# Last chunks without folds, coarser norm bound, nine early units and another split of the output stores in a fused attention and convolution kernel

## The chip, the cores and the metric

The kernel runs on one core of one Trainium2 chip, in float32. The metric is the device time of one launch in microseconds; the time of a version is the median of its runs.

## What is computed

The reference chains two layers over an image batch x of 2 images, 256 channels, 64 by 64 pixels:

```python
# layer 0: global attention, 8 heads of 32, over all 4096 pixels of an image
q = proj(Wq, bq) / sqrt(32); k = proj(Wk, bk); v = proj(Wv, bv)
fuse = softmax(q @ k.T) @ v
hybrid = conv1x1(concat([x, fuse]), Wf, bf)
x = hybrid * m + x * (1 - m)             # m: mask, 32x32 resized to 64x64
# layer 1
x = x * sigmoid(channel_mlp(x))
x = x + window_attention(x)              # 8x8 windows, 4 heads of 64
x = channel_shuffle(x, 4)
y = relu(bn(grouped_conv7x7(x, sa_w1)))  # 64 groups: 4 channels to 1
y = bn(grouped_conv7x7(y, sa_w2))        # 1 channel to 4
out = x * sigmoid(y)
```

## The kernel before, in words

**Start.** The images are cut into 16 chunks of 512 pixels (2 images, 8 chunks each). For each chunk TensorE computes q and k (line 435), ScalarE adds the bias and squares them (445 to 448), and VectorE takes the maximum of the squares over groups of 4 tokens (454). One chunk later `norms` (411 to 416) sums these maxima over the 32 rows of each head with a 0/1 matrix on TensorE (4 matmuls) and VectorE keeps the largest. The result bounds every score, and a flag (498) decides whether the exponentials need a shift; the two versions of the rest are built as `arm("a")` and `arm("b")`, and with these inputs the flag takes arm a, without the shift. Then the v projection runs (472).

**Attention.** `slots` lists image, chunk, half of the heads g and key block m: 64 slots for a chunk. In each slot TensorE computes scores (640), ScalarE exponentiates (653), TensorE multiplies by v (691), and VectorE adds the exponentials up (697). In all chunks but the last there are two chains of sums, one for even and one for odd m (`chains = 2`), joined at the end (699). `fold` (661) then packs the sums of a chunk, [128, 4, 512] for each g, with 24 DMAs on GpSimd into one tile (tag "w0"), so that the denominators need 3 terms of 4 small matmuls (725); in the last chunk, with one chain, they are computed from the sums themselves in 8 terms. Their reciprocal (752) goes to DRAM and comes back spread over the rows (737, 744), and VectorE multiplies the attention output by it (758). `at(delay, action)` puts such actions off by a number of slots.

**Stages.** The rest of layer 0 and layer 1 up to the shuffle of a chunk is the generator `stage`. It is advanced every fourth slot, so it runs beside the next chunk's attention. It begins with the 1x1 convolution (`hya`, 526), whose first half needs only x and whose second half needs the multiplied attention output `fa`, and it ends with rows written to the DRAM array `xs` (1020). The last chunk's stage has no attention beside it.

**Convolutions.** `convolve` is a generator as well. A unit u is 4 groups. An item of `items` is a unit with one or both images. For each item `conv1` (1088) and `conv2` (1113) run on TensorE, ScalarE makes the gate of it (1124, 1130), and `gate` (1136) multiplies it with x (1141) and stores it to the output: 12 DMAs for each image, dealt out over the issuing engines in `engines`; stores on ScalarE are held back and issued after the next item's ScalarE work (1159). After it come the loads of a later item's rows (`load_rows`, 1067) and of a later unit's weights (`load_w`, 1060). Image 0 is complete before the last chunk of image 1, so its first `EARLY` units (0 to 7) go as single-image items ahead of all that needs image 1; they fill TensorE in the last chunk's stage, one generator step at each `yield True` of `stage`, after two steps during the wait for the denominators (1261). `staged` is set when the last stage is over. Each image-1 row load waits for that stage's `xs` writes. The items are 8 singles of image 0, 6 singles of image 1 (units 2 to 7), units 8 to 15 with both images, and units 1 and 0 of image 1. Rows are loaded into 4 buffers in turn. `conv1` has one PSUM tile, so it starts when ScalarE has drained the one before (1096).

Each engine is given its instructions in a fixed order. DMAs are issued by SP, ScalarE and GpSimd, each also in order. In the built program the DMAs of SP and ScalarE share eight completion semaphores in turn and those of GpSimd have eight of their own; a DMA is not issued before the one that had its semaphore eight turns earlier has landed.

Of the kernel before, what the change touches and what calls it, by code (L numbers as in the profile page):

```python
# [31 lines left out]
DN = 8  # L32
EARLY = 8
HEADS1, HD1 = 4, 64
# [23 lines left out]
def conv_seq_kernel(ctx: ExitStack, tc: tile.TileContext, a, out):  # L58
# [311 lines left out]

    nm = const.tile([P, B * NCHUNK], F32, name="nm")
    flag = const.tile([1, 1], I32, name="flag")
    warm = const.tile([1, 1], F32, name="warm")
    with (
# [36 lines left out]
        def norms(i, tops):  # L411
            s = psum1(f"nrm_{i}")
            for n in range(2 * KC):
                s_ = s[32 * n : 32 * n + 32, 0 : CH // 4]
                nc.tensor.matmul(s_, headsum, tops[:, n, :], start=True, stop=True)
            nc.vector.tensor_reduce(nm[:, i : i + 1], s[:, 0 : CH // 4], AX.X, ALU.max)
# [6 lines left out]
        for i, (b, c) in enumerate(chunks):  # L423
            load_chunk()
            x = xs0[i]
            sq = st0.tile([P, 2 * KC, CH], F32, tag="sq", name=f"sq_{b}_{c}")
            tops = st0.tile([P, 2 * KC, CH // 4], F32, tag="top4", name=f"top4_{b}_{c}")
            for n, w in (("q", wq), ("k", wk)):
# [25 lines left out]
            nc.vector.tensor_reduce(  # L454
                tops, sq.rearrange("p g (n f) -> p g n f", f=4), AX.X, ALU.max
            )
            if i:
                norms(i - 1, last)
            last = tops
# [7 lines left out]
        for i, (b, c) in enumerate(chunks):  # L467
# [18 lines left out]
            if i == 0:  # L486
                norms(len(chunks) - 1, last)
                nc.vector.tensor_reduce(top, nm, AX.X, ALU.max)
            elif i == 1:

                nc.tensor.matmul(row[0:1, 0:P], top, ident, start=True, stop=True)
                qk2 = w0.tile([1, 2], F32, name="qk2")
                nc.vector.tensor_reduce(
                    qk2, row[0:1, 0:P].rearrange("p (i r) -> p i r", i=2), AX.X, ALU.max
                )
                prod = w0.tile([1, 1], F32, name="prod")
                nc.vector.tensor_mul(prod, qk2[:, 0:1], qk2[:, 1:2])
                nc.vector.tensor_scalar(flag, prod, (SAFE / SCALE0) ** 2, None, ALU.is_le)
            elif i == 2:


                s = psum1("bvf")
                for oc in range(KC):
                    for kc in range(KC):
                        nc.tensor.matmul(
                            s[:, oc : oc + 1],
                            wf[:, KC + kc, oc * P : (oc + 1) * P],
                            bv[:, kc : kc + 1],
                            start=(kc == 0),
                            stop=(kc == KC - 1),  # L510
                        )
                nc.vector.tensor_add(bf, s[:, 0:KC], bf)
# [17 lines left out]
    def pipeline(arm, shifted, pools):  # L530
# [145 lines left out]
        def products(i):  # L676
            b, c, g, m = slots[i]
            chains = 1 if (b, c) == (B - 1, NCHUNK - 1) else 2
            if m == 0:
                acc[0] = avp.tile([P, CH], F32, tag="av", name=f"av{arm}_{i}")  # L680
# [19 lines left out]
            if stop:  # L700
# [3 lines left out]
                nc.scalar.copy(f[:, g, :], av)  # L704
                if chains == 2:
                    fold(totals.pop((b, c, g)), b, c, g)
                if g == 0:
                    return
                both = [] if chains == 2 else [totals.pop((b, c, gg)) for gg in range(KC)]
                parts = folds.pop((b, c), [])  # L710
# [38 lines left out]
                late = EB + 1 if (b, c) == (0, 0) else 0  # L749
                wait = DN + 2 * (chains == 2)  # L750
                at(wait, denominators)
# [276 lines left out]

        items = [(u, (0,)) for u in range(EARLY)] + [(u, (1,)) for u in range(2, EARLY)]
        items += [(u, (0, 1)) for u in range(EARLY, NU)] + [(1, (1,)), (0, (1,))]  # L1030
        staged, held = [], deque()

        def convolve():
# [102 lines left out]
            def gate(k, zs):  # L1136
                u, images = items[k]
                for m, b in enumerate(images):
# [3 lines left out]

                    engines = (nc.gpsimd, nc.sync)
                    if k >= len(items) - 2:
                        engines = (nc.scalar, nc.sync)
                    elif staged and k < EARLY:
                        engines = (nc.gpsimd, nc.scalar)
                    stores = 0
# [18 lines left out]
            def more():  # L1167
                if staged and not xcs:
# [5 lines left out]
                    xcs.append(pool.tile([P, B * nb, UG, WP], F32, name=f"xl{arm}3"))  # L1174
                    load_rows(EARLY + 3)
                return bool(xcs)
# [9 lines left out]
            for k, (u, images) in enumerate(items):  # L1186
# [10 lines left out]
                if xcs or k + 4 < EARLY:  # L1197
                    load_rows(k + 4)

# [27 lines left out]
        for i, (b, c, g, m) in enumerate(slots):  # L1227
            now[0] = i
            if (b, c, g, m) == (B - 1, NCHUNK - 1, 0, 16):
                for _ in banded:  # L1230
                    pass
                conv = convolve()
                next(conv)
# [10 lines left out]
            if g == KC - 1 and m == NMB - 1:  # L1244
                late = EB + 4 if (b, c) == (0, 0) else 0
                at(DN + 8 + ((b, c) != (B - 1, NCHUNK - 1)) + late, lambda b=b, c=c: stages.append(stage(b, c)))
            run_later()
# [10 lines left out]
        while later:  # L1258
            now[0] += 1
            run_later()  # L1260
            if now[0] in (len(slots) + DN, len(slots) + DN + 1):
                next(conv)
# [91 lines left out]
```

## Time and profile before

| | us |
|---|---|
| median of 3 runs (2928.01 to 2930.89) | 2930.63 |
| profiled execution, own time | 2927.96 |
| its span, first to last instruction | 2926.2 |
| TensorE busy | 2873.4 (98%) |
| ScalarE busy | 2455.0 (84%) |
| VectorE busy | 2437.0 (83%) |
| GpSimd busy | 568.6 (19%) |

The span was cut for reading at the ends of stages: projections to 186 us, attention with stages from there to 2696, the last stage with single units to 2762, the remaining convolutions to 2910, and the last stores to 2926. A line of the timeline is start, duration, engine, source line, operation and tile, and in brackets the idle time before it with what ended it. "issue" there means that the engine waited for nothing that the profile shows. SPq and ACTq lines are the DMA issues on these queues; their length covers waits between the DMAs of one group.

### The profile page before, as it was taken

Reading aid. Unit: us, or ns where it says so; the run is one execution under the profiler, and the core shown is the slowest. Engines: PE = TensorE matmul, PEld = TensorE weight load, DVE = VectorE, ACT = ScalarE, POOL = GpSimd, SP = SyncE. Lnnn points to the kernel's source line nnn. Section 1 sums busy time; section 2 is a strip of 40 time slices with the busy share of each in tenths; the row PEclk is TensorE's granted clock in tenths of the full one; section 3 lists DMA queues with packets and bytes.
Section 4 is the critical chain, followed back from the end, with each engine's and each line's share of the span. In section 5 each row is a group of like instructions: output and inputs, shape, how many; then the busy total and the mean of one; then the engine's idle time right before and its main releaser. Section 6 shows DMA issues by size and latency. Waiting matters only on the chain.

```text
span 2926.2 us, 84951 instructions
## 1 busy us (share of the span) xinstructions
PE 2873.4 (98%) x36722; PEld 821.6 (28%) x36722; DVE 2437.0 (83%) x1356; ACT 2455.0 (84%) x4143; POOL 568.6 (19%) x929
## 2 busy tenths in 40 slices
PE   9999999999999999999999999999999999999897
PEld 3551122222222222222222222222222222223564
DVE  4339999899999999989989999999999998988211
ACT  5569989898989898989989898989898998978433
POOL 8111111111011212121111101111212121100356
PEclk9999999999999999999999999999999999999999
DMA  8545433333343434343333334343434343332564
GB/s 246 202 172 186 147 89 75 95 83 89 69 95 78 105 79 104 79 91 89 91 86 82 88 73 92 72 97 79 106 77 91 88 97 84 86 103 81 154 202 108
DMA packets 249364, 307.71 MB, mean 105 GB/s; under 512 B 124432, under 2 KB 141012, under 8 KB 248724
## 3 DMA queue, kind: packets, MB, share of 16 engines
q1 hardware_dynamic: 200996, 231.74, 27.8%
q0 software_dynamic: 40656, 67.09, 12.3%
q8 instruction: 291, 4.77, 0.7%
q10 hardware_dynamic: 7328, 3.36, 0.5%
q14 instruction: 93, 0.76, 0.1%
HBM read 221.88 MB, written 66.39 MB: 99 GB/s over the span
## 4 chain that ended last, share of the span: by engine, by line
PE 91%; DMA 3%; DVE 2%; issue 2%; ACT 1%; POOL 1%; SPq 0%; ACTq 0%; DVEq 0%; POOLq 0%
PE sa L640 34%; PE ava L691 33%; PE qka L526 4%; PE hya L526 3%; PE c1a L1088 2%; PE c2a L1113 2%; PE vwa L526 2%; PE opa L526 2%; PE v L472 2%; PE q L435 2%; PE k L435 1%; DVE suma L697 1%; DMA invs<-inva 1%; PE sca L878 1%; PE oa L972 1%
## 5 line engine op out<-in xcount | busy, mean ns | idle before, releaser
L653 ACT ACTIVATE ea<-sa 128x512 f32<-128x512 f32 (+1 forms) x3072 | 2037.1, 747 | 49.4 <-PE sa L640 22.6
L640 PE MATMUL sa<-qa,ka 32*64 32x512 f32 x16384 | 1146.6, 613 | 1.5 <-ACT vst L480 1.2
L697 DVE TENSOR_TENSOR suma<-suma,ea 128x2048 f32<-128x2048 f32 x480 | 1097.6, 2287 | 5.8 <-DVE suma L697 0.5
L691 PE MATMUL ava<-ea,va 128*32 128x512 f32 x8192 | 1091.1, 605 | 1.0
L697 DVE TENSOR_TENSOR odda<-odda,ea 128x2048 f32<-128x2048 f32 x420 | 959.7, 2285 | 46.0 <-ACT ea L653 45.9
L670 POOL DMA_DIRECT2D folda<-suma x360 | 252.7, 899 | 1787.7 <-DVE suma L699 1043.2
L640 PEld LDWEIGHTS sa<-qa,ka 32*64 32x64 f32 x16384 | 242.4, 129 | 785.5 <-ACT ea L653 716.5
L691 PEld LDWEIGHTS ava<-ea,va 128*32 128x32 f32 x8192 | 161.6, 108 | 834.0 <-issue 804.6
L697 DVE TENSOR_TENSOR suma<-ea,ea 128x2048 f32<-128x2048 f32 x32 | 73.2, 2286 | 58.8 <-ACT ea L653 58.8
L1161 POOL DMA_DIRECT2D out_dram<-za x180 | 101.7, 573 | 86.0 <-DVE za L1141 63.6
L526 PE MATMUL qka<-ua,qkv_w 128*32 128x512 f32 x1024 | 116.2, 592 | 0.3 <-DVE ua L834 0.3
L781 ACT ACTIVATE ta<-hya,bf 128x512 f32<-128x512 f32 x32 | 20.3, 685 | 108.9 <-PE hya L526 102.9
L1141 DVE TENSOR_TENSOR za<-za,xla 128x768 f32<-128x768 f32 x24 | 23.0, 959 | 100.6 <-ACT za L1130 88.7
L454 DVE TENSOR_REDUCE top<-sq 128x512 f32<-128x2048 f32 x16 | 36.6, 2285 | 79.3 <-ACT sq L448 79.3
L737 POOL DMA_DIRECT2D invs<-inva x62 | 34.3, 562 | 296.0 <-DVE inva L752 295.0
L899 ACT ACTIVATE ewa<-ewa,mxwa 128x64 f32<-128x64 f32 x256 | 85.5, 350 | 1.5 <-DVE mxwa L890 1.5
L1113 PE MATMUL c2a<-yca,wa 32*64 32x192 f32 (+1 forms) x2688 | 83.3, 384 | 0.7 <-issue 0.5
L785 DVE TENSOR_TENSOR ta<-ta,mca 128x512 f32<-128x512 f32 x32 | 22.0, 689 | 71.4 <-ACT ta L781 71.4
L1124 ACT ACTIVATE za<-c2a 128x384 f32<-128x384 f32 x64 | 27.9, 487 | 57.0 <-PE c2a L1113 30.1
L1088 PE MATMUL c1a<-xla,wa 128*32 128x192 f32 (+1 forms) x896 | 64.1, 435 | 11.6 <-issue 5.9
L857 ACT ACTIVATE qka<-qka,qkv_b 128x512 f32<-128x512 f32 x64 | 40.4, 685 | 40.8 <-PE qka L526 40.8
L1020 POOL DMA_DIRECT2D xs<-xo x94 | 72.0, 1017 | 11.0 <-DVE xo L1005 8.3
(143 smaller groups left out, 1724.7 us busy)
## 6 DMA issues: line engine op xcount, KB each, us to landing
ka<-ks SPq DMA_DIRECT2D x256, 256.0 KB
va<-vs SPq DMA_DIRECT2D x256, 256.0 KB
folda<-suma POOLq DMA_DIRECT2D x240, 64.0 KB, 3.1
folda<-suma POOLq DMA_DIRECT2D x120, 128.0 KB, 3.9
wa<-ws SPq DMA_DIRECT2D x17, 896.0 KB
ws<-zeros SPq DMA_DIRECT2D x16, 896.0 KB
xs<-xo POOLq DMA_DIRECT2D x78, 140.0 KB, 7.9
xla<-xs SPq DMA_DIRECT2D x24, 420.0 KB
```

What stands on the lines that cost most here:

```text
L435: nc.tensor.matmul(s[:, g, :], w[:, kc, g * P : (g + 1) * P], rhs, start=(kc == 0), stop=(kc == KC - 1),)
L526: nc.tensor.matmul(out[o : o + 32], weights[:, o : o + 32], x, start=start, stop=stop)
L640: nc.tensor.matmul(heads[j][o], k[r, cols][:, o], q[r, g, :], start=True, stop=not shifted)
L653: nc.scalar.activation(e[:, h, :], tile, AF.Exp, scale=SCALE0)
L670: nc.gpsimd.dma_start(dst[p : p + rows], total[rows * k : rows * k + rows, h, :], accum_op=ALU.add if k else ALU.bypass,)
L691: nc.tensor.matmul(av[r, :], v[:, m % PB, r], e[:, j, :], start=start, stop=stop)
L697: nc.vector.tensor_add(total, first.pop(m % chains, total), e)
L899: nc.scalar.activation(e[:, n, :], e[:, n, :], AF.Exp, bias=mx[:, n : n + 1], accum_out=rs[:, n : n + 1],)
L1020: eng.dma_start(x_s[b, n, p + r0 : p + r1].rearrange("r g w -> g r w"), xo[64 * h : 64 * h + 64, oc, r0 - WS * c : r1 - WS * c, :],)
L1088: nc.tensor.matmul(s[32 * j : 32 * j + 32, 0 : n * W], w[:, j, d, :], xs[k][:, 0:n, j, d : d + W], start=(d == 0), stop=(d == KS - 1),)
L1113: nc.tensor.matmul(tiles[j // 2][o, j % 2, 0 : n * W], w[r, d, o], y[r, 0:n, d : d + W], start=(d == 0), stop=(d == KS - 1),)
L1161: eng.dma_start(*args)
```

## The change

It touches four places.

- The squares are reduced over 16 tokens instead of 4, four chunks share one `tops` tile, and `norms` runs once for four chunks: 4 times instead of 16.
- `folded` replaces the test on `chains`: chunk 6 of image 1 keeps its two chains but is no longer folded, its denominators come from the sums, 2 slots earlier; the due time of its stage moves by one slot. `convolve` is started at slot 12 of the last chunk instead of 16.
- `EARLY` is 9: unit 8 becomes two single items. The last unit, 15, becomes two single items too. There is one more generator step during the last wait for denominators. At the staging, the rows of one image-1 item are loaded instead of four, and later ones at most one item for each gate until the ninth.
- Stores: of each three, two go to GpSimd and one to SP; none to ScalarE, except in the last two items (before: in items 4 to 7 and the last two).

```diff
-EARLY = 8
+EARLY = 9
...
-    nm = const.tile([P, B * NCHUNK], F32, name="nm")
+    nm = const.tile([P, B * NCHUNK // 4], F32, name="nm")
...
-                nc.tensor.matmul(s_, headsum, tops[:, n, :], start=True, stop=True)
+                nc.tensor.matmul(
+                    s_, headsum, tops[:, n].rearrange("p c n -> p (c n)"), start=True, stop=True
+                )
...
-            tops = st0.tile([P, 2 * KC, CH // 4], F32, tag="top4", name=f"top4_{b}_{c}")
+            if i % 4 == 0:
+                tops = st0.tile([P, 2 * KC, 4, CH // 16], F32, tag="top16", name=f"top16_{i}")
...
-                tops, sq.rearrange("p g (n f) -> p g n f", f=4), AX.X, ALU.max
+                tops[:, :, i % 4], sq.rearrange("p g (n f) -> p g n f", f=16), AX.X, ALU.max
             )
-            if i:
-                norms(i - 1, last)
+            if i and i % 4 == 0:
+                norms(i // 4 - 1, last)
...
-                norms(len(chunks) - 1, last)
+                norms(len(chunks) // 4 - 1, last)
...
+            folded = (b, c) < (B - 1, NCHUNK - 2)
...
-                if chains == 2:
+                if folded:
                     fold(totals.pop((b, c, g)), b, c, g)
...
-                both = [] if chains == 2 else [totals.pop((b, c, gg)) for gg in range(KC)]
+                both = [] if folded else [totals.pop((b, c, gg)) for gg in range(KC)]
...
-                wait = DN + 2 * (chains == 2)
+                wait = DN + 2 * folded
...
-        items += [(u, (0, 1)) for u in range(EARLY, NU)] + [(1, (1,)), (0, (1,))]
+        items += [(u, (0, 1)) for u in range(EARLY, NU - 1)]
+        items += [(NU - 1, (0,)), (NU - 1, (1,)), (1, (1,)), (0, (1,))]
...
-                    engines = (nc.gpsimd, nc.sync)
-                    if k >= len(items) - 2:
+                    engines = (nc.gpsimd, nc.gpsimd, nc.sync)
+                    if k == len(items) - 1:
                         engines = (nc.scalar, nc.sync)
-                    elif staged and k < EARLY:
-                        engines = (nc.gpsimd, nc.scalar)
+                    elif k == len(items) - 2:
+                        engines = (nc.scalar, nc.sync, nc.sync)
...
-                    load_rows(EARLY + 3)
+                    load_rows(EARLY)
...
-                    load_rows(k + 4)
+                    load_rows(min(len(xs) + (k >= EARLY - 1), k + 4))
...
-            if (b, c, g, m) == (B - 1, NCHUNK - 1, 0, 16):
+            if (b, c, g, m) == (B - 1, NCHUNK - 1, 0, 12):
...
-                at(DN + 8 + ((b, c) != (B - 1, NCHUNK - 1)) + late, lambda b=b, c=c: stages.append(stage(b, c)))
+                at(DN + 8 + ((b, c) < (B - 1, NCHUNK - 2)) + late, lambda b=b, c=c: stages.append(stage(b, c)))
...
-            if now[0] in (len(slots) + DN, len(slots) + DN + 1):
+            if len(slots) + DN <= now[0] <= len(slots) + DN + 2:
                 next(conv)
```

## The prediction

> **What bounds the kernel now.** I read the stage table (busy time by stretch) first, then TensorE's timeline at every stage where it isn't full, then the chain of waits there, then the queues that the change touches.
>
> ```profile
> 186.00:2525.00 2339.00, 2332.32 (x29461) 548.98 (x29465) 2180.99 (x1134) 2131.38 (x3604) 363.98 (x546) 1.00 0.39 93
> 2525.00:2583.00 58.00, 53.94 (x608) 11.86 (x600) 50.24 (x25) 43.03 (x67) 15.94 (x26) 0.97 0.58 143
> 2762.00:2779.20 17.20, 11.27 (x337) 9.44 (x329) 3.21 (x4) 4.01 (x8) 8.27 (x14) 0.94 0.68 190
> 2779.20:2820.60 41.40, 35.54 (x1008) 28.52 (x1008) 5.76 (x6) 12.72 (x25) 20.32 (x36) 0.86 0.65 178
> 2897.30:2926.20 28.90, 12.71 (x395) 10.19 (x392) 5.14 (x6) 8.34 (x16) 13.51 (x24) 0.78 0.33 60
> ```
>
> The first busy column is TensorE. It is full for 2339 us of attention, which the change doesn't touch: no more than the start and the last 400 us can move. There TensorE loses 4 us, 6 us, 6 us and 16 us. Its timeline names the holes:
>
> ```profile
> 14.25 3.60 PE L435 MATMUL q<-x,WqT 128*128 128x512 f32 x8
> 48.31 3.60 PE L435 MATMUL k<-x,WkT 128*128 128x512 f32 x8
> 51.84 0.43 PE L415 MATMUL nrm<-top,headsum 128*32 128x128 f32 x8
> 52.20 3.70 PE L435 MATMUL q<-x,WqT 128*128 128x512 f32 x8
> 2570.40 3.62 PE L526 MATMUL hya<-xa,WfT 128*32 128x512 f32 x32
> 2578.07 5.34 PE L526 MATMUL hya<-fa,WfT 128*32 128x512 f32 x32 [4.05 <-DVE fa L758]
> 2715.30 5.34 PE L526 MATMUL hya<-fa,WfT 128*32 128x512 f32 x32 [2.63 <-DVE fa L758]
> 2779.20 4.71 PE L1088 MATMUL c1a<-xla,wa 128*32 128x192 f32 x56 [5.73 <-ACT yca L1096]
> 2813.34 4.64 PE L1088 MATMUL c1a<-xla,wa 128*32 128x192 f32 x50 [4.49 <-issue]
> ```
>
> Twice `hya` waits for the multiplied attention output. The first image-1 convolution waits for ScalarE; the chain there shows what ScalarE itself stood behind, a store on its queue that was released as a row load landed:
>
> ```profile
> 2772.16 6.17 DMA xla<-xs
> ...
> 2778.36 0.32 ACTq L1159
> ...
> 2778.72 0.43 ACT yca L1096
> ```
>
> At the end the last matmul stops at 2910.3, but stores run on, on two queues:
>
> ```profile
> 2897.68 23.04 SPq L1161 DMA_DIRECT2D out_dram<-za  x36
> 2915.25 7.43 ACTq L1159 DMA_DIRECT2D out_dram<-za  x12
> ```
>
> **What the Trainium skill says.** "TensorE: Matmul & The Clock Gate", What's actually happening: an idle window of about 3.4 us halves TensorE's clock until a busy window has passed. The trace agrees in kind: the same `hya` half takes 3.62 us after work, but 5.34 after holes of 4.05 and even 2.63 us; `conv1` 4.71 instead of 2.53 after 5.73. "Runtime: NRT & Kernel Launch", Instruction fetch mechanics: an engine's instructions come in blocks of 256 by its own DMA queue. The trace agrees: the instruction queue moved 4.77 MB in 291 packets, 16.4 KB each, and between the "issue" stops that end at 2805.10 and 2813.34 there are 127 matmuls and 128 weight loads, 255 instructions. "DMA: Bandwidth & Descriptors", Issuing engines are not separate DMA queues: another issuing engine saves issue time, not transfer time. So the store split is worth only waits in queues.
>
> **The change, part by part**, as TensorE time against the span of 2926.2.
>
> *Norms.* A chunk with one starts every 7.42 us (52.20 less 44.77, the q before); without, k to q and q to k are 3.43 each (10.82, 14.25, 17.68), 6.86. A norm costs 0.56. Of the 12 removed, those after chunks 1 to 3 give nothing: at chunk 4 the remaining one still waits for chunk 3's maximum, which ends at 44.28 because ScalarE stood behind weight DMAs (4.25 us at 37.35). The one before the v projection gives nothing either: the last norm waits 0.85 us for VectorE there already. 8 count: 8 x 0.56 = 4.5. TensorE, earlier at chunk 4, now idles some 2.3 us before that norm instead of 0.88; a slow clock after it costs 0 to 1.9 (3.62 to 5.34, rounded up). I take 1.0. A reduction over 16 isn't in the trace: it reads the same 2048 elements (2.29 us); between half and twice that it stays hidden, as chunks are 6.86 apart and it is due one chunk later. Twelve 0.28 us reductions on VectorE go, hidden. **-3.5**.
>
> *Unfolded chunk 6.* 24 GpSimd DMAs (0.90 us each) go, beside other work. Denominators take 64 matmul passes (1.94 us, the last chunk's) instead of 24 (0.84): +1.1 on TensorE. They come 2 slots earlier, and VectorE reaches the reciprocal after 8 sums instead of 10; a sum takes 2.39 there (21.46 for 9), so at 2557.1, not 2561.8. Its round trip took 12.9 us from the reciprocal's end (2562.75) to the last landing (2575.67); again 12.9 gives 2571; VectorE reaches `fa` after 14 sums at 2572.4 and ends at 2573.6. TensorE, with +1.1, wants it at 2575.1. So the wait of 4.05 goes, and the slow clock after it (5.34 less 3.62 = 1.7). The row loads of the convolution now start near 2552 instead of 2561, ahead of two k and v pieces; 2.6 MB at the 280 GB/s seen in 2560 to 2570 is 9 us, and the pieces are needed at slot 18, after 2575. The same loads hit the round trip in both kernels. Chunk 6's sums stay in two of three buffers until then; the next claim on them is slot 32, so nobody waits. VectorE follows: its 6.18 us wait in this stage shrinks by as much. **-4.7**.
>
> *Last stage.* `conv2(1)` (2.57 us) now stands before `hya`, so the 2.63 us hole is filled and the slow half (1.7) goes. ScalarE has one gate less between `ca1` and `ca2`, where TensorE waited 1.05: I take 0.7. **-5.0**. All of `conv1(8)`, `conv2(7)` then lies between `op` and the first image-1 item.
>
> *Staging.* That hole of 5.73 and its slow `conv1` (4.71 less 2.53 = 2.2) lose both causes: ScalarE's queue holds no stores, and one row load of 420 KB is in flight, not four (6.17 us together). From `op` TensorE has 3 `conv2` and 2 `conv1`, 12.7 us; `xs` and the issue took 9.2 us from 2762.0 to 2771.2. GpSimd now has 8 stores before its two `xs` writes; 8 x 0.57 = 4.5 us fits in the 7 us of `o`, `conv1(6)` and `op`. With 3 to 4 us for landing the hole is 0 to 2; I take 0.8. On SP the new load waits ahead of 8 stores of items 5 and 6; their buffers are wanted four items later, 20 us. **-7.1**.
>
> *Split units.* 2 units x (2 x 2.47 - 4.74 + 2 x 2.57 - 4.80) = **+1.1**.
>
> *Single-item stretch.* Two "issue" stops (1.37 and 4.49) and the slow clock after them cost 8. Row and weight loads there come at 1.3 to 1.7 MB in 5 us. After, five singles have both loads instead of four, but the load begins lighter. TensorE needs 256 instructions every 3.8 us here; the two blocks before the stops came after some 5 and 8. From gone (-8) to all late (+12), I take **0**.
>
> *Stores and end.* Single items: 8 x 0.57 = 4.6 us on GpSimd of 5.04; both images: 16, 9.1 of 9.54. It keeps up. From the end of matmuls, 2910.3, to 2926.2 is 15.9. ScalarE's first held store was late because SP, with 36 stores at 0.64, held the semaphores. After, SP has 4, 4, 8 and 6 in the last four items, so ScalarE starts 1.8 us after the matmuls, issues 10 at 0.5 (0.42 unhurried, 0.62 here) and lands 3.5 later (2922.7 to 2926.2): 10.3. **-5.6**.
>
> The sum is -3.5 - 4.7 - 5.0 - 7.1 + 1.1 + 0 - 5.6 = -24.8: a span of 2901.4, an own time 1.8 more (2927.96 less 2926.2), 2903.2. The median of the runs stood 2.7 above the profiled execution (2930.63 less 2927.96): 2906.
>
> **The rivals.** *Late instructions:* single items and loads overlap for longer, and blocks come late through all of it, +12: 2918. For it: both stops lie where the DMA share is 0.9; against: doubles at 0.8 show none. *The round trip is late anyway:* earlier row loads hold up inv and rd, the 4.05 us wait stays, +4.7: 2911. *Stops gone too:* -8 and a full clock at the start, -1: 2897. *The GpSimd store stream becomes the bound*, slower: from the fifth gate to item 23 there are 200 stores on GpSimd. That gate comes 57 us into the tail (from `conv1(0)` at 2696.3; 2764.2 is 68 now, less 5.0, less the 6 of `op` and `conv1(6)` that now follow it). It decides above 0.77 us a store, where 57 + 200 x 0.77 + 3 for landing = 214, the tail that I expect (229.9 less 16.6). `folda` issues took 0.90, and GpSimd also waits for its semaphores when a landing takes longer than issuing 8. At 0.95 the tail is 250, not 213: 2943, +12 on before. Against it: 180 stores took 0.573. *The change doesn't do what it says:* a looser norm bound could send the kernel to the shifted arm; I computed 40,800 against the limit of 115,200, so no.
>
> **How the numbers follow.** Forecast 0.58 (2906, itself 2900 to 2912), late instructions 0.15, late round trip 0.10, stops gone 0.12, store stream 0.05. 2896 to 2919 leaves out the store stream and the outer parts of the second and fourth. A measurement can tell 0.2%, 6 us, from no change: faster 0.93, same 0.02 (the upper end of late instructions), slower 0.05.
>
> **What would show it.** 4 `nrm` groups, chunks 6.86 apart; no wait at the second `hya` half near 2570 and in the last stage, both at 3.6 us; no ACTq stores before the last two items; first `xla` convolution within 2 us of `conv2(7)`; GpSimd stores at 0.57; some 10 us from last matmul to end. The forecast is wrong if TensorE's "issue" time in the single items exceeds 15 us, or if GpSimd's stores run on after SP's.

## The result, and the profile after

The changed kernel took 2915.9 us (median of 6 runs, 2910.0 to 2918.8) against 2930.8 for the kernel before: a ratio of 0.9949, interval 0.9936 to 0.9962. The profiled execution took 2910.0, its span 2908.0, so 18.2 us less than the span before. The forecast was 2906 in a range of 2896 to 2919, and a span of 2901.4: the sign and the range held, but 6.6 us of the 24.8 that the sum promised for the span didn't come, and 10 by the medians, for the profiled execution was the fastest of the six.

The stage table of the changed kernel, cut at the same events (columns: stretch, length, then busy time of TensorE, of its weight loads, of VectorE, ScalarE and GpSimd, the granted clock, the DMA share, GB/s):

```profile
181.00:2521.00 2340.00, 2332.10 (x29460) 548.43 (x29448) 2180.44 (x1134) 2130.60 (x3604) 351.42 (x530) 1.00 0.40 92
2521.00:2579.00 58.00, 57.99 (x704) 13.73 (x704) 53.69 (x30) 47.55 (x74) 10.63 (x18) 1.00 0.52 126
2750.80:2765.64 14.84, 13.99 (x450) 11.96 (x449) 3.21 (x4) 5.72 (x11) 9.87 (x17) 1.00 0.59 142
2765.64:2810.80 45.16, 40.23 (x1181) 33.47 (x1178) 6.71 (x7) 15.04 (x29) 31.95 (x58) 0.96 0.73 207
2892.60:2908.00 15.40, 0.02 (x4) 0.00 (x0) 0.96 (x1) 1.63 (x3) 4.26 (x8) 0.61 0.30 55
```

TensorE is now full at chunk 6 and nearly full at the staging. It still loses 5 us among the single items of image 1, and 15.4 us pass between the last matmul and the end, as before (15.9). Its timeline, at the places shown of before:

```profile
43.32 0.43 PE L415 MATMUL nrm<-top,headsum 128*32 128x128 f32 x8 [1.82 <-DVE top L457]
...
2571.04 3.62 PE L529 MATMUL hya<-fa,WfT 128*32 128x512 f32 x32
...
2706.44 3.62 PE L529 MATMUL hya<-fa,WfT 128*32 128x512 f32 x32
...
2765.64 2.54 PE L1093 MATMUL c1a<-xla,wa 128*32 128x192 f32 x56
...
2802.97 0.63 PE L1118 MATMUL c2a<-yca,wa 32*64 32x192 f32 x11 [2.18 <-issue]
2803.53 4.19 PE L1093 MATMUL c1a<-xla,wa 128*32 128x192 f32 x56
```

No bracket stands behind the two `hya` halves and the first image-1 convolution: the three holes are gone, and so are the slow halves (3.62 for 5.34, 2.54 for 4.71). The first norm group waits 1.82 us. The queues at the end:

```profile
2878.83 18.04 POOL L1166 DMA_DIRECT2D out_dram<-za  x32 [0.49 <-issue]
```

```profile
2881.35 20.73 SPq L1166 DMA_DIRECT2D out_dram<-za  x22
```

```profile
2896.33 6.96 ACTq L1164 DMA_DIRECT2D out_dram<-za  x10
```

SP does have 22 stores where it had 36, but ScalarE's ten begin 3.7 us after the last matmul (2892.6), not 1.8, and take 0.70 us each. GpSimd, which stood idle between items before, has hardly a pause left (0.5 us). Before, it had this:

```profile
2897.94 6.76 POOL L1161 DMA_DIRECT2D out_dram<-za  x12 [2.80 <-DVE za L1141]
2905.21 6.76 POOL L1161 DMA_DIRECT2D out_dram<-za  x12 [0.52 <-DVE za L1141]
```

The chain of waits, which ended in ScalarE and VectorE before, now ends on GpSimd (columns: start, us, what):

```profile
2891.25 0.53 issue
2891.78 4.51 POOL out_dram L1166 x8
2896.29 0.01 POOLq L1290
2896.30 0.57 POOL out_dram L1166
```

This view starts from the last busy instruction, and the DMA issues of SP and ScalarE don't count as busy. It stops 11 us before the span ends, so it can't say by itself what sets the end.

Where the 18.2 us of span are, with the prediction's terms beside them. The sums at chunk 6 and in the tail are made as in the prediction: a single item of image 0 (5.04 us) that has moved ahead of the image-1 items is counted with the items, and the slow clock after a hole with the hole.

| step | predicted | in the profile after |
|---|---|---|
| norms (first attention matmul at 180.46, before 185.98) | -3.5 | -5.5 |
| attention to 2521 | 0 | +1.6 |
| chunk 6 (the `opa` before it to the `opa` after it) | -4.7 | -4.9 |
| last stage and staging together | -12.1 | -12.0 |
| split units and single items, to the last matmul | +1.1 | +3.1 |
| stores and end | -5.6 | -0.5 |
| sum | -24.8 | -18.2 |

### The profile page after: what moved, and what is told of

The parts are those of the page before. It is cut to its first block, busy times and chain, and to the rows that moved or that the text cites. A ratio compares the mean times of both kernels' runs of the same rounds, so it can differ in the third digit from the quotient of the medians.

```text
span 2908.0 us, 85469 instructions
## 1 busy us (share of the span) xinstructions
PE 2864.2 (98%) x37002; PEld 828.2 (28%) x37002; DVE 2435.1 (84%) x1344; ACT 2455.7 (84%) x4145; POOL 584.8 (20%) x965
## 3 DMA queue, kind: packets, MB, share of 16 engines
q0 software_dynamic: 41360, 66.48, 12.7%
## 4 chain that ended last, share of the span: by engine, by line
PE 89%; DMA 4%; POOL 3%; issue 1%; DVE 1%; ACT 1%; ACTq 0%; SPq 0%; DVEq 0%; POOLq 0%
PE sa L643 35%; PE ava L695 33%; PE qka L529 4%; PE hya L529 3%; POOL out_dram L1166 2%; PE vwa L529 2%; PE opa L529 2%; PE v L475 2%; PE q L438 1%; PE k L438 1%; PE c2a L1118 1%; PE c1a L1093 1%; DMA invs<-inva 1%; PE sca L882 1%; DMA folda<-suma 1%
## 5 line engine op out<-in xcount | busy, mean ns | idle before, releaser
L673 POOL DMA_DIRECT2D folda<-suma x336 | 235.5, 891 | 1664.0 <-DVE suma L703 980.0
L1166 POOL DMA_DIRECT2D out_dram<-za x240 | 135.7, 573 | 51.7 <-DVE za L1146 26.6
L457 DVE TENSOR_REDUCE top<-sq 128x128 f32<-128x2048 f32 x16 | 36.6, 2284 | 74.5 <-ACT sq L451 74.5
L1118 PEld LDWEIGHTS c2a<-yca,wa 32*64 32x64 f32 x2912 | 68.1, 191 | 24.5 <-issue 17.3
```

Of the source, the lines that this page charges most:

```text
L673: nc.gpsimd.dma_start(dst[p : p + rows], total[rows * k : rows * k + rows, h, :], accum_op=ALU.add if k else ALU.bypass,)
L1118: nc.tensor.matmul(tiles[j // 2][o, j % 2, 0 : n * W], w[r, d, o], y[r, 0:n, d : d + W], start=(d == 0), stop=(d == KS - 1),)
L1166: eng.dma_start(*args)
```

## The experiments

Theory, from this table: the mechanisms of the prediction hold up to the last matmul; what is missing is mostly the end, and it is missing because something other than SP's 36 stores sets it. My first candidate was the set of eight completions that SP and ScalarE share: all 24 stores of the last two items lie on them. The rivals: GpSimd's stream of stores, which has hardly a pause left; the landings themselves; and that the parts are worth other amounts than the table says. Twelve kernels ran, in three groups, each beside the kernel before on one chip. The median of the kernel before was 2926.1, 2929.5 and 2923.7 us in the groups, so only ratios of one group are compared closely.

### The parts alone

**Norms alone.** The kernel before with these lines:

```diff
-            tops = st0.tile([P, 2 * KC, CH // 4], F32, tag="top4", name=f"top4_{b}_{c}")
+            if i % 4 == 0:
+                tops = st0.tile([P, 2 * KC, 4, CH // 16], F32, tag="top16", name=f"top16_{i}")
...
-            if i:
-                norms(i - 1, last)
+            if i and i % 4 == 0:
+                norms(i // 4 - 1, last)
```

> The kernel before with the coarser norm bound alone (squares reduced over 16 tokens, 4 norm groups instead of 16). Theory now, from the trace after: the start gives about 6.5 us (the stage table of after stands 6.57 us ahead at its first attention stage), of which up to 2.7 can be given back by chance at waits for the landing of the spread reciprocals, so a ratio of 0.998 to 0.9985 (4 to 6.5 us). The prediction's own step: 3.5 us, ratio 0.9988, with a slow clock of 1 us after the first norm's wait. Rival: the lead is lost again at the first wait for a DMA in attention, ratio 1.000.

Measured: ratio 0.9966 (0.9956 to 0.9977), about 10 us. In its profile the first attention matmul is 6.1 us earlier, and 3.1 us more come in the last stage, which this kernel doesn't change:

```profile
2708.18 3.64 PE L529 MATMUL hya<-fa,WfT 128*32 128x512 f32 x32 [1.71 <-DVE fa L761]
...
2769.22 4.69 PE L1091 MATMUL c1a<-xla,wa 128*32 128x192 f32 x56 [5.48 <-ACT yca L1099]
```

The hole that was 2.63 us is 1.71 here, and no slow half follows it: that is 0.9 and 1.7 us that the edit wasn't made for. Another 4.7 us of this profile come after that stage, and no run explains them. The staging hole stands as before. Over all kernels of this study the first attention matmul starts at 179.9 to 182.0 us with the coarser bound (10 profiles) and at 185.8 to 188.1 without (4): means 181.2 and 186.7, 5.5 us apart. The step of -3.5 was too small; the rival that the lead is lost at once falls.

**Chunk 6 alone.**

```diff
+            folded = (b, c) < (B - 1, NCHUNK - 2)
...
-                if chains == 2:
+                if folded:
                     fold(totals.pop((b, c, g)), b, c, g)
...
-            if (b, c, g, m) == (B - 1, NCHUNK - 1, 0, 16):
+            if (b, c, g, m) == (B - 1, NCHUNK - 1, 0, 12):
```

> The kernel before with chunk 6 of image 1 unfolded and the convolution's first loads at slot 12 instead of 16, alone. The prediction's step and the theory now agree: the wait of 4.05 us at the second half of the 1x1 convolution near 2570 goes, and its slow half (5.34 to 3.6), against 1.1 us more denominators: -4.7, ratio 0.9984. Rival: the lead is lost at the staging, where the first image-1 row load waits for DMA landings and not for TensorE: ratio 1.000 with the wait gone near 2570 all the same.

Measured: 0.9969 (0.9957 to 0.9981). Between the `opa` of chunk 5 and that of chunk 6 this kernel, and every other one with the edit (10 profiles), gained 4.86 or 4.87 us against the kernel before. The kernels without it have a wait of 4.05 us there, the same in all four profiles. The step is right. The rest of this kernel's gain is again a shorter hole in the last stage (2.27 us, no slow half) and, after that stage, 5.9 us that no run explains.

**Stores alone.**

```diff
-                    engines = (nc.gpsimd, nc.sync)
-                    if k >= len(items) - 2:
+                    engines = (nc.gpsimd, nc.gpsimd, nc.sync)
+                    if k == len(items) - 1:
                         engines = (nc.scalar, nc.sync)
-                    elif staged and k < EARLY:
-                        engines = (nc.gpsimd, nc.scalar)
+                    elif k == len(items) - 2:
+                        engines = (nc.scalar, nc.sync, nc.sync)
```

> The kernel before with the new dealing of the stores alone (two of three on GpSimd, no ScalarE before the last two items). The prediction's steps: the end 5.6 us shorter and the hole at the staging shorter by what ScalarE's stores add there, together -6 to -10, ratio 0.9966 to 0.998. Theory now: the end is not shorter, since the 24 stores of the last two items all lie on SP and ScalarE, whose eight shared completions give back one store in 0.46 us while landings take 3 to 4 us, and only the staging gains about 1 us (the row load in front of it still lands late, four loads in flight): -1 to -2, ratio 0.9995. Rival: GpSimd's stream (0.563 us a store, 16 of 9.54 us in a double item) falls behind and the whole tail gets longer, ratio over 1.001.

Measured: 0.9997 (0.9988 to 1.0005): nothing. But it is a sum of two things. The first image-1 convolution waits 1.57 us, not 5.73, and runs at full clock:

```profile
2778.16 2.54 PE L1088 MATMUL c1a<-xla,wa 128*32 128x192 f32 x56 [1.57 <-DMA xla<-xs]
```

So the staging gains 4.4 us, and 2.2 more from the clock, where I had expected 1. The last matmul comes only 4.1 us earlier than before, as the attention began 2.1 us later here and other stretches differ. Then the end takes 19.2 us for 15.9:

```profile
2892.88 17.09 POOL L1161 DMA_DIRECT2D out_dram<-za  x30
...
2910.49 4.53 POOL L1161 DMA_DIRECT2D out_dram<-za  x8 [0.52 <-issue]
```

The last matmul ends at 2906.2; GpSimd stores until 2915.0, and the span runs on to 2925.4, though SP and ScalarE have issued their last at 2917.9. The shared completions don't explain these last 7.5 us.

**Items alone.**

```diff
-EARLY = 8
+EARLY = 9
...
-        items += [(u, (0, 1)) for u in range(EARLY, NU)] + [(1, (1,)), (0, (1,))]
+        items += [(u, (0, 1)) for u in range(EARLY, NU - 1)]
+        items += [(NU - 1, (0,)), (NU - 1, (1,)), (1, (1,)), (0, (1,))]
...
-                    load_rows(EARLY + 3)
+                    load_rows(EARLY)
```

> The kernel before with the items alone changed (nine single units of image 0, last unit as two, one row load at the staging instead of four, one more generator step in the last wait). The prediction's steps: last stage -5.0 and split units +1.1 fully, the staging's 7.1 only as far as it comes from the four loads in flight: with all of it -11, ratio 0.9962. Theory now: the last stage gives its 4 to 5, and of the staging about 4, since ScalarE's queue still holds stores there: -7, ratio 0.9976. Rival: ScalarE's stores alone make that hole, so the staging gives nothing: -3, ratio 0.999.

Measured: 0.9986 (0.9979 to 0.9992). The last stage has no hole (its `hya` runs through), and the staging hole is 3.29 us, still behind ScalarE. But this run doesn't test one row load instead of four. Its SP queue issues four in one go, as the kernel before does (at 2771.21), because with the old dealing SP has no stores to issue between them:

```profile
2768.13 2.03 SPq L1068 DMA_DIRECT2D xla<-xs  x4
```

In the changed kernel the stores on SP keep the loads apart:

```profile
2760.57 0.38 SPq L1072 DMA_DIRECT2D xla<-xs  x1
2761.05 5.24 SPq L1166 DMA_DIRECT2D out_dram<-za  x8
2766.33 0.39 SPq L1072 DMA_DIRECT2D xla<-xs  x1
```

The hole is shorter mainly because TensorE has one `conv2` (2.64 us) more to do ahead of it: the first image-1 convolution begins 16.1 us after the end of `op`, against 17.2 before and 12.8 in the kernel with the stores alone. A new wait eats some of the gain:

```profile
2894.80 2.55 PE L1089 MATMUL c1a<-xla,wa 128*32 128x192 f32 x56 [3.62 <-DMA xla<-xs]
```

The last item's rows are late, which with the whole change costs only 0.84 us.

**Norms and chunk 6 together**, without the other two parts:

```diff
-EARLY = 9
+EARLY = 8
...
-                    engines = (nc.gpsimd, nc.gpsimd, nc.sync)
+                    engines = (nc.gpsimd, nc.sync)
```

> The kernel before with the coarser norm bound and the unfolded chunk 6, without the new items and the new dealing of stores. By the two parts' own runs (0.9966 and 0.9969) the ratio would be 0.9935, as good as the whole change, so the tail's two parts would be worth nothing. Theory now: those two runs also held what a run can win by chance (the hole in the last stage was 1.7 and 2.3 us there, short of a slow clock, 2.6 and slow in the profile of before); of the parts themselves 5.5 to 6 and 4.9, plus up to 3 in the last stage, so 11 to 14 us, ratio 0.9952 to 0.9962, with the hole of 5 to 7 us at the staging still there.

Measured: 0.9965 (0.9952 to 0.9979), about 10 us (10.9 between the medians), just outside the 11 to 14 that I expected. That is no more than each of the two gave alone, so each of those gains held something that can't be had twice. The last stage is part of it: here too its hole is short (1.60 us) and no slow half follows. The two profiles with the coarser bound and the old items have holes of 1.60 and 1.71 us there, the three without the coarser bound 2.27 to 2.63; whether that is luck stays open. The profile has the staging hole of 6.05 us with a slow convolution of 4.71, and a last matmul only 12.4 us earlier than before (17.7 with the whole change).

### The end

**The changed kernel again**, no edit.

> The changed kernel once more, unchanged, for comparison on the same chip and for a second profile of it. If its wider spread (2910 to 2919 in six runs) comes from instruction stops of TensorE among the single items, then the profile's time stands above or below 2910.0 by what these stops differ from the first profile's 7.3 us (TensorE issue idle from 2743 to 2811). Rival: the spread comes from the waits for the spread reciprocals in attention, and the stops are the same.

Measured: 0.9939 (0.9926 to 0.9952), 2910.7 us, profiled 2911.1. The instruction stops among the single items sum to 7.3 us against 7.35 in the first profile, and the waits in attention to 4.8 us against 4.65. But the two profiled executions lie only 1.1 us apart, so this pair can't tell what spreads the runs over 11 us. What does differ is the start (182.0 for 180.5) and the end (14.1 for 15.4).

**The stores of the kernel before** in the changed kernel (the diff of "stores alone", reversed).

> The changed kernel with the dealing of the stores of the kernel before (alternately GpSimd and SP, GpSimd and ScalarE for the early items after the staging, ScalarE and SP in the last two). The prediction's steps: the end 5.6 us longer and part of the staging's hole back, so 6 to 10 us above the changed kernel. Theory now: the end is as long as in the changed kernel (about 15.5 us after the last matmul), since both have 24 stores on SP and ScalarE in the last two items; at the staging ScalarE's stores return, 0 to 4 us. Rival: the new dealing is a loss, and this kernel is faster than the changed one by over 2 us.

Measured: 0.9957 (0.9943 to 0.9971), beside 0.9939 in the same group, which the intervals can't separate. The profiled span is 4.9 us longer than that of the changed kernel in the same group, and not at the end, which takes 13.7 us (14.1). Part of it was expected: four row loads go out close together again, and the staging has a hole of 1.84 us behind ScalarE and a slow convolution after it (4.01). The larger part is one that neither theory had, a row load that waits on SP:

```profile
2879.41 5.81 SPq L1166 DMA_DIRECT2D out_dram<-za  x12
2885.32 0.39 SPq L1072 DMA_DIRECT2D xla<-xs  x1
```

```profile
2890.36 4.19 PE L1093 MATMUL c1a<-xla,wa 128*32 128x192 f32 x56 [3.60 <-DMA xla<-xs]
```

With 12 stores of each double item instead of 8, SP issues the last row load at 2885.32 (2879.83 in the changed kernel), 1.4 us before TensorE wants the rows; it costs 3.60 and a slow convolution, 1.65 more. The changed kernel waits 0.84 there. This is what its dealing buys, besides a ScalarE that is free at the staging: GpSimd takes stores that would stand ahead of a row load on SP.

**Alternate stores**: from the items with both images on, alternately GpSimd and SP, and the last item on three engines.

```diff
+                    if k >= 2 * EARLY - 2:
+                        engines = (nc.gpsimd, nc.sync)
                     if k == len(items) - 1:
-                        engines = (nc.scalar, nc.sync)
-                    elif k == len(items) - 2:
-                        engines = (nc.scalar, nc.sync, nc.sync)
+                        engines = (nc.scalar, nc.sync, nc.gpsimd)
```

> The changed kernel with stores alternately on GpSimd and SP from the first item with both images on, and the last item's on ScalarE, SP and GpSimd in turn. Theory now (the end is bound by eight completions shared by SP and ScalarE, and GpSimd's own eight stand unused because GpSimd is still behind with older stores): GpSimd has caught up by the last item, SP and ScalarE have 14 stores in the last two items instead of 24, and the end shrinks from 15.4 us after the last matmul to about 12: 3 to 4 us faster than the changed kernel. The prediction's step (10.3 us) would be met at best. Rival: the end is set by how long the last landings take and by the drain after them, whichever queue they are on: no difference.

Measured: 0.9953 (0.9938 to 0.9967), not faster. SP and ScalarE have issued their last store 6.8 us after the last matmul, 3.8 earlier than in the first profile of the changed kernel, and still the end takes 14.1. So my theory falls: the shared completions aren't what set the end of this kernel. (The late row load is back too, 3.44 us.)

**Last two items on three engines**, nothing else:

```diff
                     if k == len(items) - 1:
-                        engines = (nc.scalar, nc.sync)
+                        engines = (nc.scalar, nc.sync, nc.gpsimd)
                     elif k == len(items) - 2:
-                        engines = (nc.scalar, nc.sync, nc.sync)
+                        engines = (nc.scalar, nc.sync, nc.gpsimd)
```

> The changed kernel with only the last two items' stores dealt over ScalarE, SP and GpSimd in turn, GpSimd's backlog left as it is (two of three in all items before). SP and ScalarE have 16 stores there instead of 24 and are done about 3.5 us earlier; GpSimd, behind until 4.3 us after the last matmul, adds 8 stores of 0.57: 8.9 us after it, and lands 2 to 3.4 later, so an end of 14 to 15 us against 15.4: 0 to 1.5 us faster than the changed kernel. If the eight shared completions alone set the end, as fast as the kernel with alternate stores (3 to 4 us).

Measured: 0.9961 (0.9948 to 0.9974), and an end of 19.7 us, longer by 4 to 6 us instead of shorter:

```profile
2884.67 22.02 POOL L1166 DMA_DIRECT2D out_dram<-za  x39
```

```profile
2898.38 6.81 ACTq L1164 DMA_DIRECT2D out_dram<-za  x8
```

ScalarE is done at 2905.2, GpSimd at 2906.7; the span ends at 2917.2. What lies between is in the trace as GpSimd's closing drain: an instruction at the end of the program, filed under the `with` line around the whole kernel and not counted as busy, so that the views used so far don't list it. SP and ScalarE have closing drains too, of at most 0.1 us each; SP's comes after the last landing. This is the second theory, formed here: the end is the later of two chains, (1) SP's and ScalarE's last stores, their landing and these engines' drains, (2) GpSimd's last store, 0.9 to 3.1 us, and its drain of 5.3 to 7.9 us (the spread over all profiles). Apart from the end, attention took 5.6 us longer here than in the first profile of the changed kernel, 3.4 of it two slow halves of `hya` after waits of 2.13 and 2.69 us. All times from the end of the last matmul:

| kernel | GpSimd's last store | its drain ends | SP, ScalarE issued | their drains end | span ends |
|---|---|---|---|---|---|
| before | 1.7 | 11.0 | 12.4 | **15.1** | 15.9 |
| changed | 4.2 | **14.5** | 10.7 | 13.4 | 15.4 |
| changed, again | 4.3 | **13.2** | 10.0 | 12.8 | 14.1 |
| stores alone | 8.8 | **18.4** | 11.7 | 14.5 | 19.2 |
| old stores | -5.2 | 3.2 | 9.7 | **12.5** | 13.7 |
| alternate | 5.5 | **13.2** | 6.8 | 10.4 | 14.1 |
| last two on three | 9.2 | **18.8** | 7.7 | 12.2 | 19.7 |
| free end (below) | 2.3 | 8.5 | 10.2 | **12.9** | 13.7 |
| one store (below) | 4.0 | 11.6 | 10.2 | **12.8** | 13.6 |

The later drain is bold. In the five rows where it is GpSimd's, the span ends 0.8 to 0.9 us after it, in the four others 0.8 to 1.2 us. In three of the five the two chains are far apart (2.8 us and more); in the changed kernel they end close together, 1.1 and 0.5 us apart in its two profiles. The five profiles that the table leaves out fit as well.

**GpSimd free at the end**: a version made to beat both kernels.

```diff
+                if k >= 2 * EARLY - 2:
+                    load_rows(k + 4)
                 for m, b in enumerate(images):
...
+                    if 2 * EARLY - 2 <= k < len(items) - 4:
+                        engines = (nc.gpsimd, nc.sync)
                     if k == len(items) - 1:
-                        engines = (nc.scalar, nc.sync)
+                        engines = (nc.scalar, nc.scalar, nc.sync)
                     elif k == len(items) - 2:
-                        engines = (nc.scalar, nc.sync, nc.sync)
+                        engines = (nc.sync,) * 10 + (nc.gpsimd,) * 2
```

> The changed kernel with GpSimd out of the way at the end: alternate stores in the items with both images, two of three on GpSimd in the two items after them, then 10 on SP and 2 on GpSimd, then 8 on ScalarE and 4 on SP; and from the items with both images on the next row load is issued ahead of the stores. Theory now (the end is bound by GpSimd's closing drain, 5.7 to 7.9 us, which starts 1.7 to 3.1 us after its last store): GpSimd's last store ends about 0.8 us after the last matmul, SP and ScalarE issue until 6.5 to 8 us after it, so the span ends 11 to 12.5 us after the last matmul against 14.1 to 15.4, and the last row load is not late (no wait of 0.8 to 3.6 us at the last item): 3 to 5 us faster than the changed kernel, ratio to before 0.992 to 0.993. Rival: the eight completions shared by SP and ScalarE set the end, with 22 stores on them in the last two items instead of 24: at most 1 us faster.

Measured: 2904.4 us, 0.9940 (0.9927 to 0.9954), the same as the changed kernel in its two groups. The late row load is gone (no wait at all before the last item's convolution), and GpSimd's drain ends 4 us before those of SP and ScalarE. But the end is 13.7 us, not 11 to 12.5: now the first chain sets it. SP's first three stores of the last-but-one item landed 3.6 to 4.0 us after their issue and held the shared completions; the last ten landed in 1.5 to 2.1. Here the rival was right.

**One store moved**: the same with the very last store on GpSimd.

```diff
-                        engines = (nc.scalar, nc.scalar, nc.sync)
+                        engines = (nc.gpsimd,) + (nc.sync, nc.scalar, nc.scalar) * 3 + (nc.sync, nc.scalar)
```

> The same with the very last store on GpSimd instead of ScalarE, a single DMA of 24 KB. Theory now: GpSimd's last store then ends some 3.3 us after the last matmul, its drain at 12.5 to 14, and the span 13.5 to 15 after the last matmul: 2 to 3 us later than with that store on ScalarE. Rival (landings or the shared completions set the end): no later, or 0.4 us earlier, as ScalarE has one store less.

Measured: 0.9943 (0.9929 to 0.9956), an end of 13.6 us: no later. GpSimd's drain did move from 8.5 to 11.6, but the other chain was still at 12.8. The 2 to 3 us that I expected rested on SP and ScalarE having issued all by 8; they hadn't. So this run confirms the two chains only in so far as the shorter one costs nothing.

### The instruction stops

**Fewer loads**: the changed kernel without the row loads of the image-1 items of units 6 to 8.

```diff
+                    if EARLY + 4 <= k < 2 * EARLY - 2:
+                        continue
                     nc.sync.dma_start(
```

> The changed kernel without the row loads of the last three single items of image 1 (units 6 to 8; they compute with rows left in the buffers, so these outputs are wrong data). These loads of 420 KB go out near 2782, 2788 and 2794. If TensorE's instruction stops come late because instruction blocks share the DMA engines with row loads, the stops at the same instructions near 2782 and 2788 (1.17 and 1.56 us in the changed kernel; 17 and 58 matmuls left of the group) shrink below 0.3 us, and the one near 2803 (2.18; 11 left), with loads for the first item of both images, stays at 1.9 to 2.7. Rival: a block takes its time whatever the load, then all three stay between 0.5 and 2.7.

Measured: 0.9959 (0.9946 to 0.9972). The stops stayed:

```profile
2778.51 0.76 PE L1120 MATMUL c2a<-yca,wa 32*64 32x192 f32 x17 [0.92 <-issue]
2784.55 1.60 PE L1120 MATMUL c2a<-yca,wa 32*64 32x192 f32 x58 [1.27 <-issue]
2790.76 2.45 PE L1120 MATMUL c2a<-yca,wa 32*64 32x192 f32 x98 [1.58 <-issue]
```

They are 0.92 and 1.27 us, for 1.17 and 1.56: the theory that row loads make them falls, at least for these loads (the DMA share from 2776 to 2811 was 0.71 instead of 0.78). All stops among the single items sum to 9.0 us here, against 7.35. Their places are more telling than their sizes: 17 and 58 matmuls before the end of a group in both kernels. Counted in TensorE's instructions, those of its sequencer included, the five longest stops of the changed kernel from the last stage on lie 767, 1281, 255 and 768 apart, which is 3, 5, 1 and 3 times 256 to within 1. "Runtime: NRT & Kernel Launch" in the Trainium skill, Instruction fetch mechanics, has blocks of 256 instructions; the trace agrees with the grid. What makes one block late and another not stays open.

## Why the prediction was right, and where it was wrong

**Norms, -3.5: mis-sized, -5.5.** The terms that failed are the two for chunk 4. The slow clock of 1.0 us after the longer wait didn't come: the norm group waited 1.82 us, not 2.3, and q after it took 3.63 us. And the first norm group itself stands 1.1 us earlier than before (43.32 for 44.42), where I had given the removal after chunks 1 to 3 nothing (over all profiles the means are 44.0 and 45.1). The 8 x 0.56 stand.

**Attention, 0: not forecast.** Waits of the second `hya` half for `fa` occur at the same places (near 830, 1306 and 2254 us in the changed kernel) and sum to 4.65 us against 2.39 before. Without the coarser bound they sum to 1.5 to 2.6 us (4 profiles), with it to 1.1 to 4.8 (10). So some of the start's lead may be given back here; no run tested it, and the spreads overlap.

**Chunk 6, -4.7: right**, -4.86 or -4.87 in ten profiles. The wait of 4.05 and its slow half went, the extra denominators stayed.

**Last stage and staging, -5.0 and -7.1: right as a sum**, -12.0, though it holds 2.4 us of new instruction stops. The staging hole is gone altogether, where 0.8 was left, but partly because the work ahead of it took 14.8 us instead of 12.7: the rows were there only 14.6 us after the end of `op` (issued at 9.8, landed in 4.8; the step had 9.2 and 3 to 4). Of the two causes that the step named for the hole of 5.73, the runs bear out one. Without ScalarE's stores, and with four row loads still in flight, 1.57 is left. In the kernel before, ScalarE's held stores went out at 2774.51, 2775.73 and 2778.36, as the first, second and third row load landed, whose completions they share; the work that TensorE needed stood behind them. The other cause, four loads instead of one, isn't shown: no run changes it alone, and the first load took 3.2 to 4.7 us to land where four went out together (7 profiles) and 3.3 to 4.8 where one did (7). The 1.57 that was left is covered by the one `conv2` more. What the last stage is worth varies with the hole that it fills: 1.6 to 2.6 us in five profiles without the edit, with a slow half after it in two.

**Split units +1.1, single items 0: +3.1 together.** The stops and the slow clock were taken as 8 before and 8 after. After the first image-1 convolution the stops are 4.9 us and one slow convolution 1.7, before 5.9 and 2.4. What outweighs that is the late last row load, 0.84, and groups that ran long without a stop in the profile (`c2a` up to 3.2 us for 2.64).

**Stores and end, -5.6: the step that failed**, -0.5. Its sum was 1.8 + 5.0 + 3.5 = 10.3 us, and the end took 15.4. "ScalarE starts 1.8 us after the matmuls": it started after 3.7, because its first store needs a completion that SP's store of 2892.27 held until 2896.25, a landing of 4.0 us. "Issues 10 at 0.5": the ten took 0.70 each, 7.0 in all. The 3.5 for landing was about right, though not for its reason: the last ten stores landed in 1.6 to 2.2, and ScalarE's drain and the close came after. These three put the end at about 14.3 (an estimate: ScalarE's drain ended at 13.4, and the span ends at least 0.8 after it in the other profiles). So some 3.9 of the missing 5.1 us are ScalarE's late start and slow stores. The rest, some 1.1 (0.5 by the same estimate in the second profile), is a cost that the step put at nothing. It took GpSimd to "keep up": it kept up with issuing (0.563 us a store), but without a pause, so its last store came 4.2 us after the last matmul instead of 1.7, and its drain ended last. The profile of before held a drain of 7.5 us as well, from 3.6 to 11.0 us after the last matmul, hidden under SP's 36 stores; I read what these stores covered on the other queues and not what they covered at GpSimd's end.

The rival of GpSimd's stream was right in its place and wrong in its price: it decided at 0.77 us a store, through the buffers, and a store took 0.563; by the estimate above the stream cost 0.5 to 1.1 us at the end instead (4 to 7 with the stores alone and with the last two items on three engines). A condition under which the forecast called itself wrong, GpSimd's stores running on after SP's, didn't occur; its drain did. The median fell by less than the profiled span (14.8 and 18.2 us), but in the second group by 18.8. That the whole came within 6.6 us of the sum is in part luck: norms and chunk 6 gave 2.2 us more than their steps said, against 8.8 us that went missing elsewhere.

## What to carry to other kernels

The end of a program has its own ledger: for each queue that issues DMAs, the last issue, its landing and the engine's closing drain, and only the latest counts. In these profiles GpSimd's drain ended 6 to 10 us after its last store, so a kernel that stores through GpSimd should have its last store there that much earlier than the other queues are done. Ask what each moved store stood ahead of: here the dealing paid at the staging, where it left ScalarE free, and for a row load on SP, not at the end. Look in the trace whether a part alone still does what it does in the whole: the items alone issued four row loads at once. And a hole in TensorE's work can be worth its own length or 1.7 us more, depending on which side of about 2.2 us it falls, so a part measured alone can win by the way what another part wins by design.

## What the runs showed of the hardware

- GpSimd's closing drain took 5.3 to 7.9 us in all 14 profiles, and started 0.9 to 3.1 us after its last store (all these kernels store through GpSimd, so none shows it without). "Perfetto Trace Analysis" in the Trainium skill, DMA Instruction — SWDGE (GPSIMD), says that the record of a DMA issued by GpSimd ends when its descriptors are generated, not when the data has moved; the trace agrees (the last store's record ends at 2896.87, its last completion comes at 2899.72).
- The clock of TensorE after a wait of the second `hya` half, over 46 waits in 14 profiles: up to 2.12 us the half took 3.64 us always, from 2.13 to 2.27 twice 3.64 and twice 5.34, from 2.47 on 5.34 or more always. "TensorE: Matmul & The Clock Gate", What's actually happening, has some 3.4 us of idle; here less suffices, and the measurement decides.
- Landings of SP's stores (24 or 16 KB) come in quick and slow stretches: 1.5 to 1.9 us for most of those issued from 2897 to 2904 in the kernel before, 4.2 in the changed kernel at 2882 and at 2893, with GpSimd storing in all three. In the changed kernel those issued just after GpSimd's last store still took 2.6 to 3.3, and those issued after that store had landed (2899.72) were quick, 1.6 to 2.2. What makes a stretch slow stays open.
